# Keys and values of an attention context by seven half-block products instead of eight (f32, one Trainium2 core)

## The chip, the cores and the metric

The kernel runs on one core of one Trainium2 chip. The metric is the time on the device in microseconds (us), as the median of several runs. All arithmetic is f32.

## What is computed

A block of a network with cross attention, for one sequence of T = 4096 rows, H = 512 features, 8 heads of 64, and a context of S2 = 3202 rows. Cut to what matters:

```
x      = layernorm(builder_state); base_n = layernorm(ctx)            # rows of 512
q      = x @ Wq.T + bq;  k = base_n @ Wk.T + bk;  v = base_n @ Wv.T + bv
attn   = softmax(q k^T / 8) per head;  x = residual + (attn v) @ W_o.T + b_o
U      = (layernorm(x) @ W_in.T + b_in) @ Bmat
s_t    = silu(s_{t-1} @ A.T) + U_t                                    # a scan over t
result = x + s @ Cmat + mean(program_probs) @ W_prog.T + b_prog
```

The change touches only how k and v are formed: two products of the normalized context (3202 x 512) with 512 x 512 weights.

## The kernel before

The program has a first stage, which forms keys and values of the whole context and writes them to the chip's memory (`kd`, `vd`), and a long second stage, the attention and all that follows, whose instructions stand in an order that a planner wrote out by hand-set costs and due times (`Plan`). The second stage loads keys and values back in pieces (`load_k`, `load_v`, in SyncE's DMA queue, called SP).

In the first stage the context is cut into 26 chunks of 128 rows (the last has 2 rows), and the chunks into groups of GC = 4, so 512 keys a group. There are six full groups, 0 to 5, and a seventh with chunks 24 and 25.

- `load_chunk` (L566) loads a chunk by an SP DMA into `cx`, a ring of six.
- `norm_chunk` (L573) normalizes it: statistics on VectorE, three small operations on GpSimd, then one ScalarE instruction that writes `xh` (L288).
- `turn_chunk` (L592) transposes `xh` by four TensorE transposes into PSUM and copies them into `ct`, the group's 128 x 4 x 512 tile of features by keys: with VectorE for odd chunks, with ScalarE for even ones.
- For the first two chunks of groups 2 to 5 (`flips`, L605) TensorE is spared: `flip_pair` transposes 32 x 32 blocks on VectorE into a tile `pair`, and `move_pair` puts them in their place in `ct` by 16 SP DMAs, in four parts of four (L562).
- Values: for each chunk, four matmuls of 512 columns into a PSUM bank `pv` (L673), a ScalarE copy to `vs`, a store to `vd`.
- Keys: after a group's last chunk, for each of the four head pairs, four matmuls of 512 columns (all keys of the group) into a bank `pk` (L709), a ScalarE copy with bias to `ks`, two stores to `kd`.

PSUM has two banks each for `pk`, `pv` and the transposes. Each engine, and SP's queue, works through its instructions in the order in which the program gives them.

Beside this runs `side()` (a generator, `work`): weight preparation, row biases, and the first block of queries (`first_queries`). `next(work)` lets it run to its next `yield`; the code places these calls between the chunks and the key blocks, 70 of them, where 52 are enough to finish.

Of the kernel before, what the change touches and what calls it, by code (L numbers as in the profile page):

```python
# [10 lines left out]
F32 = mybir.dt.float32  # L11
BF16 = mybir.dt.bfloat16
I32 = mybir.dt.int32
AF = mybir.ActivationFunctionType
ALU = mybir.AluOpType
# [40 lines left out]
def keys(c):  # L56


    return CK if c < NCH - 1 else REST


def blocks(c):

    return 2 if c < NDC - 1 else 1


def key0(c):
    return c * CK


class Plan:
# [22 lines left out]
    def __init__(self, rings, held):  # L94
        self.rings = rings
        self.taken = {r: list(held.get(r, ())) for r in rings}
        self.pieces, self.givers = {}, {}
# [94 lines left out]
def xattn_ssm_kernel(  # L192
# [219 lines left out]
    def gain(k, w, i=None):  # L412
        for i in range(NC) if i is None else (i,):
            nc.vector.tensor_scalar(
                w[:, i, :], raw[k][:, i, :], g1s[:, i : i + 1], None, ALU.mult
            )
# [29 lines left out]
    def side():  # L446
# [14 lines left out]
        nc.scalar.dma_start(cb, ctxb[:a, :].rearrange("(p c) d -> p c d", p=P))  # L461
        cb2 = wp.tile([S2 - a, NS], F32, name="cb2")
        nc.scalar.dma_start(cb2, ctxb[a:, :])
        x0 = wp.tile([P, NT, H], F32, tag="raw_v", name="x0")
        yield

        nc.vector.tensor_scalar(bias[:, :NC], bias[:, :NC], HD**-0.5, None, ALU.mult)
# [47 lines left out]

        sums = wp.tile([P, NS], F32, name="sums")
        nc.vector.tensor_reduce(sums, cb.rearrange("p c d -> p d c"), AX.X, ALU.add)
        nc.scalar.dma_start(x0, x[:QB, :].rearrange("(t p) h -> p t h", p=P))
        yield
        pm = m_tile([P, 512], "pm")  # L520
# [45 lines left out]
    def load_chunk(c):  # L566
        if c < NCH:
            n = keys(c)
            xt = cin.tile([CK, H], F32, tag="cx", name=f"cx_{c}", bufs=6)
            nc.sync.dma_start(xt[:n], ctx_in[key0(c) : key0(c) + n, :])  # L570
            cxs[c] = xt

    def norm_chunk(c):  # L573
        if c < NCH:
            xhs[c] = normalize(cxs.pop(c), keys(c), f"c{c}", pool=cin)
# [16 lines left out]
    def turn_chunk(c):  # L592
        if c < NCH:
            g, n = c // GC, keys(c)
            if c % GC == 0:
                cts[g] = ctp.tile([P, NC, GC * CK], F32, tag="ct", name=f"ct_{g}")
            o = key0(c) - key0(g * GC)
            copy = nc.vector.tensor_copy if c % 2 else nc.scalar.copy
            tp = transposes(kps, "t", xhs.pop(c), n, f"c{c}")
            for cs in (slice(0, 2), slice(2, NC)) if c == 0 else (slice(0, NC),):  # L600
                copy(cts[g][:, cs, o : o + n], tp[:, cs])  # L601
# [3 lines left out]
    def flips(c):  # L605
        return FLIPS <= c // GC < NCH // GC and c % GC < 2

    def flip_pair(c):
        g = c // GC
        pairs[g] = wp.tile([P, NC, H], F32, tag="raw_" + "vqkq"[g - FLIPS], name=f"pair_{g}")  # L610
        for t in range(2):
            flip(pairs[g][:, :2], xhs.pop(c + t), t)

    def move_pair(c, *parts):
        g = c // GC
        if 0 in parts:
            cts[g] = ctp.tile([P, NC, GC * CK], F32, tag="ct", name=f"ct_{g}")
        for a in parts:
            move(cts[g][:, :, : 2 * CK], pairs[g][:, :2], a)

    with tc.manual_schedule():
        load_chunk(0)
        nc.scalar.dma_start(g1s, g1)
        fetch_w(2, nc.scalar, slice(0, NC // 2))
        fetch_w(2, nc.sync, slice(NC // 2, NC))
        load_chunk(1)
        load_chunk(2)
        fetch_w(1, nc.sync)
        load_chunk(3)
        idle = m_tile([P, 512], "idle")  # L630
        nc.scalar.copy(bu, neg_half)
        for _ in range(11):
            nc.tensor.matmul(idle[:, :P], a_t, a_t, start=True, stop=True)
        for t, src in ((be1s, beta1), (bqkv, b_qkv), (g2s, g2), (be2s, beta2)):
            nc.sync.dma_start(t, src)
        for c in range(4, 6):
            load_chunk(c)
        early = [first_chunk(c) for c in range(2)]
        next(early[0])
        next(early[0])  # L640
        turn_chunk(0)
        gain(2, wv, 0)
        gain(2, wv, 1)
        next(early[1])
        gain(2, wv, 2)
        norm_chunk(2)
        gain(2, wv, 3)
        next(early[1])
        work = side()
        first = shift(1)  # L650
        loads = [partial(load_k, *steps[k]) for k in range(AHEAD_K - 1)]
        loads += [partial(load_v, *steps[k]) for k in range(AHEAD - 1)]
        for c in range(NCH):
            load_chunk(c + 6)
            if c >= 2 * AHEAD_K:
                for _ in range(4):
                    if loads:
                        loads.pop(0)()
            if not flips(c + 3):
                norm_chunk(c + 3)  # L660
            elif c % GC == 1:
                norm_chunk(c + 3)
                norm_chunk(c + 4)
            if flips(c + 1) and c % GC == GC - 1:
                move_pair(c + 1, 0, 1)
            g, n = c // GC, keys(c)
            ct, o = cts[g], key0(c) - key0(g * GC)
            pv = kps.tile([P, 512], F32, tag="v", name=f"pv_{c}")
            parts = 1 if c < NCH - 1 else 2
            for i in range(NC // parts):  # L670
                for h in range(parts):
                    k = h * NC // parts + i
                    nc.tensor.matmul(  # L673
                        pv[h * HD : h * HD + n, :H],
                        ct[:, k, o : o + n],
                        wv[:, k, :],
                        start=(i == 0),
                        stop=(i == NC // parts - 1),
                        skip_group_check=True,
                    )  # L680
            if c == 0:
                turn_chunk(1)
            if not flips(c + 2):
                turn_chunk(c + 2)
            elif c % GC == 2:
                flip_pair(c + 2)
            if c < NCH - 1:
                vs = cin.tile([CK, NC, P], F32, tag="vs", name=f"vs_{c}")
                nc.scalar.copy(vs, pv)
                nc.sync.dma_start(vd[:, c // 2, :, c % 2, :].rearrange("h p d -> p h d"), vs)  # L690
            else:
                second = wp.tile([n, H], F32, name="second")
                nc.scalar.copy(second, pv[HD : HD + n])
                nc.vector.tensor_tensor(vx[:n], pv[:n], second, ALU.add)
                nc.sync.dma_start(vx[HD : HD + n], vx[:n])
            if c < GC:
                if c == 1:
                    gain(1, wk)
                for _ in range((0, 0, 1, 2)[c]):
                    next(first)  # L700
            else:
                next(work, None)
            if c % GC < GC - 1 and c < NCH - 1:
                continue
            n_g = o + n
            for hp in range(NC):
                pk = kps.tile([P, 512], F32, tag="k", name=f"pk_{g}_{hp}")
                for i in range(NC):
                    nc.tensor.matmul(  # L709
                        pk[:, :n_g],  # L710
                        wk[:, i, hp * P : (hp + 1) * P],
                        ct[:, i, :n_g],
                        start=(i == 0),
                        stop=(i == NC - 1),
                    )
                ks = cin.tile([P, GC * CK], F32, tag="ks", name=f"ks_{g}_{hp}")
                nc.scalar.activation(  # L717
                    ks[:, :n_g], pk[:, :n_g], AF.Identity, bias=bias[:, NC + hp : NC + hp + 1]
                )
                for b in range(g * GC, c + 1, 2):  # L720
                    m, k = blocks(b // 2) * CK, key0(b) - key0(g * GC)
                    nc.sync.dma_start(kd[hp, b // 2, :, :m], ks[:, k : k + m])
                if g == 0:
                    nc.gpsimd.tensor_copy(kx[:, hp, REST:], ks[:, : HD - REST])
                elif c == NCH - 1:
                    nc.gpsimd.tensor_copy(kx[:, hp, :REST], ks[:, CK : CK + REST])
                if hp < 2 and flips(c + 1):
                    move_pair(c + 1, 2 + hp)
                for _ in range(2 if g > 1 else 1):
                    next(work, None)  # L730
        left = sum(1 for _ in work)
        assert left == 0, left
    prep.close()
# [208 lines left out]
    def join(w):  # L942
        o = rows_of(w, o_t[w["at"]])
        nc.vector.tensor_tensor(o, rows_of(w, w["po"][1][:, :QU], True), o, ALU.add)
# [1080 lines left out]
```

## Time and profile before

| | us |
|---|---|
| median of 3 timed runs (1939.45, 1939.58, 1941.25) | 1939.58 |
| span of the profiled execution, first to last instruction | 1938.7 |
| the profiled execution's own time | not given apart from its span; the median lies 0.9 above the span |
| first stage, from the trace: first values' matmul, first scores | 7.5, 213.1 |
| 200 of the values' matmul instructions, busy | 90.4 |
| 192 + 32 of the keys' matmul instructions, busy | 85.1 + 3.8 |

PE is TensorE's matmuls, PEld its weight loads, DVE is VectorE, ACT is ScalarE, POOL is GpSimd, SP is SyncE, whose queue issues most DMAs. A matmul's duration in the trace includes the drain of the array and overlaps the next, so its price is read from the distance between starts. In a row of instruction groups the columns are line, engine, operation, tiles written and read, shapes, count, then busy time and mean duration in ns, then the idle time of the engine ahead of them with what ended it. A row of a timeline has the start, the length (us), the engine, the line and the count of merged instructions.

### The profile page before, as it was taken

How to read it: one execution, taken by the hardware profiler on the slowest of the kernel's cores; microseconds unless marked ns; L12 is line 12 of the kernel's file. 1: busy time of each engine (PE TensorE's matmuls, PEld its weight loads, DVE VectorE, ACT ScalarE, POOL GpSimd, SP SyncE). 2: the span in 40 equal slices, each digit the busy share in tenths (PEclk: the TensorE clock that was granted, in tenths of full speed). 3: DMA queues.
4: the chain of work that ended last, by engine and by line, in shares of the span. 5: the costliest groups of instructions: out<-in, count | busy, mean ns of one | idle time of the engine just before them, and what ended most of it. 6: DMA issues, size and time to landing. Idle time of an engine off the chain costs nothing.

```text
span 1938.7 us, 66985 instructions
## 1 busy us (share of the span) xinstructions
PE 1922.7 (99%) x29056; PEld 1275.0 (66%) x29056; DVE 1467.1 (76%) x1986; ACT 1169.3 (60%) x1626; POOL 217.2 (11%) x370
## 2 busy tenths in 40 slices
PE   9999999999999999999999999999999999999997
PEld 5444579676667666666667666766666666766675
DVE  5320489688877887888868887888788886978876
ACT  3232577576666666667657666666666765766653
POOL 2121000001200120002100120012000110011105
PEclk9999999999999999999999999999999999999999
DMA  6644234123432243233412343224323341545577
GB/s 198 196 120 113 64 87 115 47 87 88 125 87 81 84 119 77 68 96 83 124 49 87 88 126 84 82 83 120 76 73 92 81 123 58 150 115 145 171 190 227
DMA packets 260758, 207.43 MB, mean 107 GB/s; under 512 B 94632, under 2 KB 233896, under 8 KB 260460
## 3 DMA queue, kind: packets, MB, share of 16 engines
q1 hardware_dynamic: 256440, 196.48, 35.6%
q10 hardware_dynamic: 4020, 6.62, 1.1%
q8 instruction: 230, 3.77, 0.8%
q14 instruction: 68, 0.56, 0.1%
HBM read 156.32 MB, written 29.88 MB: 96 GB/s over the span
## 4 chain that ended last, share of the span: by engine, by line


## 5 line engine op out<-in xcount | busy, mean ns | idle before, releaser
L838 ACT ACTIVATE p<-s,shifts 128x1024 f32<-128x1024 f32 (+1 forms) x832 | 892.9, 1082 | 477.2 <-PE s L761 461.7
L846 DVE TENSOR_TENSOR acc<-p,acc 128x1024 f32<-128x1024 f32 (+1 forms) x704 | 828.6, 1177 | 136.2 <-ACT p L838 100.3
L761 PE MATMUL s<-q,k 64*64 64x256 f32 x12800 | 840.0, 377 | 0.2 <-ACT p L838 0.2
L895 PE MATMUL po<-p,v 64*64 64x256 f32 x12800 | 838.5, 377 | 0.0
L761 PEld LDWEIGHTS s<-q,k 64*64 64x64 f32 x12800 | 500.8, 133 | 198.9 <-ACT p L838 15.0
L895 PEld LDWEIGHTS po<-p,v 64*64 64x64 f32 x12800 | 498.0, 133 | 184.1 <-issue 17.5
L967 DVE RECIPROCAL rd<-rd 128x256 f32<-128x256 f32 (+1 forms) x64 | 110.1, 1722 | 70.9 <-ACT rd L962 70.9
L1132 POOL TENSOR_TENSOR xr<-xr,rowb 128x512 f32<-128x512 f32 x30 | 39.9, 1340 | 994.9 <-DMA xr<-in_x_dram 573.4
L333 PE MATMUL pq<-xn,wq 128*128 128x512 f32 x248 | 110.6, 598 | 0.0
L1138 PE MATMUL pa<-wo,o 128*128 128x512 f32 x240 | 107.0, 599 | 0.0
L673 PE MATMUL pv<-wv,ct 128*128 128x512 f32 (+1 forms) x208 | 92.2, 595 | 0.9 <-DVE ct L601 0.5
L709 PE MATMUL pk<-ct,wk 128*128 128x512 f32 (+1 forms) x224 | 88.9, 550 | 0.0
L846 DVE TENSOR_TENSOR acc<-p,p 128x1024 f32<-128x1024 f32 x64 | 80.3, 1254 | 10.1 <-ACT p L838 9.8
L333 PEld LDWEIGHTS pq<-xn,wq 128*128 128x128 f32 x248 | 45.7, 190 | 55.3 <-issue 55.3
L1138 PEld LDWEIGHTS pa<-wo,o 128*128 128x128 f32 x240 | 44.4, 190 | 56.0 <-issue 56.0
L601 DVE COPY ct<-tp_c 128x512 f32<-128x512 f32 (+1 forms) x9 | 5.7, 630 | 91.7 <-PE tp_c L304 91.7
L709 PEld LDWEIGHTS pk<-ct,wk 128*128 128x128 f32 x224 | 39.5, 190 | 44.5 <-issue 44.5
L673 PEld LDWEIGHTS pv<-wv,ct 128*128 128x128 f32 (+1 forms) x208 | 37.0, 186 | 44.5 <-issue 41.7
L342 ACT ACTIVATE q<-pq,bias 128x512 f32<-128x512 f32 x31 | 21.3, 688 | 73.3 <-PE pq L333 73.3
L717 ACT ACTIVATE ks<-pk,bias 128x512 f32<-128x512 f32 (+1 forms) x28 | 18.0, 642 | 72.5 <-PE pk L709 60.8
L870 DVE TENSOR_TENSOR acc<-swap,acc 64x256 f32<-64x256 f32 x126 | 53.0, 421 | 8.5 <-ACT swap L865 6.8
L865 ACT COPY swap<-acc 64x256 f32<-64x256 f32 x126 | 50.8, 403 | 7.3 <-DVE acc L853 3.9
(220 smaller groups left out, 1210.8 us busy)
## 6 DMA issues: line engine op xcount, KB each, us to landing
k<-kd SPq DMA_DIRECT2D x432, 128.0 KB, 2.3
v<-vd SPq DMA_DIRECT2D x432, 128.0 KB, 2.2
xn<-x SPq DMA_DIRECT2D x448, 32.0 KB, 1.9
xr<-in_x_dram SPq DMA_DIRECT2D x30, 256.0 KB, 3.3
x1d<-xr SPq DMA_DIRECT2D x30, 256.0 KB, 2.2
x<-in_x_dram SPq DMA_DIRECT2D x28, 256.0 KB, 3.3
cx<-in_ctx_dram SPq DMA_DIRECT2D x25, 256.0 KB, 2.9
vd<-vs SPq DMA_DIRECT2D x25, 256.0 KB, 2.5
```

Of the source, the lines that this page charges most:

```text
L333: nc.tensor.matmul(pq, wq[:, i, hp * P : (hp + 1) * P], xn[:, i, :], start=(i == 0), stop=(i == NC - 1),)
L673: nc.tensor.matmul(pv[h * HD : h * HD + n, :H], ct[:, k, o : o + n], wv[:, k, :], start=(i == 0), stop=(i == NC // parts - 1), skip_group_ ...
L709: nc.tensor.matmul(pk[:, :n_g], wk[:, i, hp * P : (hp + 1) * P], ct[:, i, :n_g], start=(i == 0), stop=(i == NC - 1),)
L761: nc.tensor.matmul(s[k0 : k0 + HD, a, b, :], kts[(*w["at"][:2], c)][r, b * CK + k0 : b * CK + k0 + HD], q[r], start=True, stop=True, skip_ ...
L838: nc.scalar.activation(t[:, :, :nb, :], w["ps"][c][:, :, :nb, :], AF.Exp, bias=w["shift"])
L846: nc.vector.tensor_tensor(w["acc"][:, :, :nb, :], t[:, :, :nb, :], before[:, :, :nb, :], ALU.add)
L865: nc.scalar.copy(w["swap"][r], of[(1 - k) * HD : (2 - k) * HD])
L870: nc.vector.tensor_tensor(of[r], w["swap"][r], of[r], ALU.add)
L895: nc.tensor.matmul(w["po"][k][a * HD : (a + 1) * HD, :QU], vts[Q, hp, c][r, b, a * HD : (a + 1) * HD], t[r, a, b, :], start=(c == 0 and b ...
L967: nc.vector.reciprocal(w["rd"][:, part], (w["pd"] if last else w["rd"])[:, part])
L1132: nc.gpsimd.tensor_tensor(v["x"], v["x"], rowb, ALU.add)
L1138: nc.tensor.matmul(v["pa"], o_t[Q, c, half][:, t * P : (t + 1) * P], wo[:, c, :], start=(c == 0), stop=(c == NC - 1),)
```

## The change

Groups 1 to 5 form keys and values by one level of Strassen's scheme (in Winograd's form). The 512 x 512 weight and the group's 512 x 512 tile are each seen as four quarters of 256 x 256 (`quarters`). Seven products of quarters and of sums of quarters give what eight products of quarters gave.

- `weight_sums` forms four sums of quarters for each weight, once, on GpSimd, in tiles of the attention's input rings. `key_sums` forms four sums of quarters of `ct` for each group on VectorE, in the ring of the queries' tiles; keys and values share them.
- A product (`Seven.product`) is four matmuls of 256 columns. Its results stay in two PSUM banks, `x` and `y`, which several products add to in turn.
- `keep` copies `x` to SBUF by ScalarE (keys: two instructions with bias; values: one). `join` adds `y` to that copy by VectorE, reading PSUM. `store` writes the finished quarter out: keys with one DMA, values with two.
- The 14 products of a group (seven for keys, a = 0, and seven for values, a = 1) stand in 14 slots in a fixed order, and the loads, norms, turns, moves and `next(work)` of the next group are hung on slots.
- Groups 0 and 6 keep the old products (`whole_chunk`, `whole_keys`). The next chunks are prepared at other places than before, `next(work)` stands at 59 places, the preloads for the second stage go out one in each slot of group 5, and the tile `x0` is taken just ahead of its load.

The diff, cut to its core:

```diff
+    def quarters(w):
+        lo, hi = slice(0, QU), slice(QU, H)
+        return w[:, :2, lo], w[:, 2:, lo], w[:, :2, hi], w[:, 2:, hi]
+    def weight_sums(w, pair):
+        a11, a12, a21, a22 = quarters(w)
+        s1, s2, s3, s4 = (t.rearrange("p (c o) -> p c o", c=2) for two in pair for t in (two[:, 0], two[:, 1]))
+        nc.gpsimd.tensor_tensor(s1, a21, a22, ALU.add)
+        nc.gpsimd.tensor_tensor(s2, s1, a11, ALU.subtract)
+        nc.gpsimd.tensor_tensor(s3, a11, a21, ALU.subtract)
+        nc.gpsimd.tensor_tensor(s4, a12, s2, ALU.subtract)
+        return dict(zip("1234567", (a11, a12, s4, a22, s1, s2, s3)))
+    def key_sums(ct, g):
+        b11, b21, b12, b22 = quarters(ct)
+        t1, t2, t3, t4 = (
+            qp.tile([P, QB], F32, tag="q", name=f"t{k}_{g}").rearrange("p (c k) -> p c k", c=2) for k in range(4)
+        )
+        nc.vector.tensor_tensor(t1, b12, b11, ALU.subtract)
+        nc.vector.tensor_tensor(t2, b22, t1, ALU.subtract)
+        nc.vector.tensor_tensor(t3, b22, b12, ALU.subtract)
+        nc.vector.tensor_tensor(t4, b21, t2, ALU.subtract)
+        return dict(zip("1234567", (b11, b21, b22, t4, t1, t2, t3)))
+    class Seven:
...
+        def product(self, k):
+            to, left, right = self.y if k in "235" else self.x, self.left[k], self.right[k]
+            for b in range(2):
+                of = slice(b * P, (b + 1) * P)
+                for i in range(2):
+                    nc.tensor.matmul(
+                        to[:, b, :],
+                        left[:, i, of] if self.of_keys else right[:, i, of],
+                        right[:, i, :] if self.of_keys else left[:, i, :],
+                        start=(k in "125" and b == 0 and i == 0),
+                        stop=(i == 1),
+                        skip_group_check=True,
+                    )
+        def keep(self, k, half):
...
+            if not self.of_keys:
+                nc.scalar.copy(t, self.x)
+                return
+            for b in range(2):
+                hp = 2 * half + b
+                nc.scalar.activation(
+                    t[:, b], self.x[:, b], AF.Identity, bias=bias[:, NC + hp : NC + hp + 1]
+                )
+        def join(self, k):
+            t = self.kept[k]
+            nc.vector.tensor_tensor(t, self.y, t, ALU.add)
+        def store(self, k, half, pair):
+            t, c, hs = self.kept.pop(k), 2 * self.g + pair, slice(2 * half, 2 * half + 2)
+            if self.of_keys:
+                nc.sync.dma_start(kd[hs, c].rearrange("h p k -> p h k"), t)
+                return
+            for j in range(2):
+                nc.sync.dma_start(vd[2 * half + j, c], t[:, :, j * P : (j + 1) * P])
+        def step(self, k):
+            self.product(k)
+            if k == "1":
+                self.keep("11", 0)
+            elif k == "2":
+                self.join("11")
+                self.store("11", 0, 0)
+            elif k == "6":
+                self.keep("12", 0)
+            elif k == "7":
+                self.keep("22", 1)
+                self.join("22")
+                self.store("22", 1, 1)
+            elif k == "4":
+                self.keep("21", 1)
+                self.store("21", 1, 0)
+            elif k == "3":
+                self.join("12")
+                self.store("12", 0, 1)
...
+        right = key_sums(cts[1], 1)
+        order = [(a, k) for k in "1265" for a in range(2)]
+        order += [(0, "7"), (1, "7"), (0, "4"), (0, "3"), (1, "4"), (1, "3")]
+        at_norm = (0, 2, 5, 8)
+        for g in range(1, NCH // GC):
+            both = [Seven(True, sums["k"], right, g), Seven(False, sums["v"], right, g)]
+            c = (g + 1) * GC
+            moved = flips(c)
+            for slot, (a, k) in enumerate(order):
+                both[a].step(k)
+                if slot in at_norm:
+                    n = c + at_norm.index(slot)
+                    norm_chunk(n)
+                    load_chunk(n + 4)
+                if moved and slot == 3:
+                    flip_pair(c)
+                elif moved and slot in (5, 7, 9):
+                    move_pair(c, *((0, 1), (2,), (3,))[(slot - 5) // 2])
+                elif not moved and slot in (4, 6):
+                    turn_chunk(c + (slot - 4) // 2)
+                if slot in (9, 11):
+                    turn_chunk(c + 2 + (slot - 9) // 2)
+                if slot == 11 and g + 1 < NCH // GC:
+                    right = key_sums(cts[g + 1], g + 1)
+                if g == NCH // GC - 1 and loads:
+                    loads.pop()()
+                if slot % 3 != 1:
+                    next(work, None)
```

In group 0 the weights' sums are formed at chunk 1 (values) and ahead of the keys (keys), and the turns of chunks 6 and 7 and the norm of chunk 7 stand between the key blocks.

More of the change, by code (lines that the diff above doesn't have):

```diff
@@ L463, in side @@
         nc.scalar.dma_start(cb2, ctxb[a:, :])
-        x0 = wp.tile([P, NT, H], F32, tag="raw_v", name="x0")
         yield
@@ L517, in side @@
         nc.vector.tensor_reduce(sums, cb.rearrange("p c d -> p d c"), AX.X, ALU.add)
+        x0 = wp.tile([P, NT, H], F32, tag="raw_v", name="x0")
         nc.scalar.dma_start(x0, x[:QB, :].rearrange("(t p) h -> p t h", p=P))
@@ new lines, in xattn_ssm_kernel, with __init__ @@
+    class Seven:
+        def __init__(self, of_keys, left, right, g):
+            self.of_keys, self.left, self.right, self.g = of_keys, left, right, g
+            tag = "k" if of_keys else "v"
+            self.x, self.y = (
+                kps.tile([P, 512], F32, tag=tag, name=f"p{tag}{k}_{g}").rearrange("p (b k) -> p b k", b=2)
+                for k in "xy"
+            )
+            self.kept = {}
+        def product(self, k):
[12 more added lines that the diff above has]
+        def keep(self, k, half):
+            t = cin.tile(
+                [P, 2, QU], F32, tag="ks" if self.of_keys else "vs", name=f"{'ks' if self.of_keys else 'vs'}_{self.g}_{k}"
+            )
+            self.kept[k] = t
+            if not self.of_keys:
[5 more added lines that the diff above has]
+                    t[:, b], self.x[:, b], AF.Identity, bias=bias[:, NC + hp : NC + hp + 1]
+                )
+        def join(self, k):
[27 more added lines that the diff above has]
+                self.store("12", 0, 1)
@@ new lines, in whole_chunk @@
+    def whole_chunk(c):
+        g, n = c // GC, keys(c)
+        ct, o = cts[g], key0(c) - key0(g * GC)
+        pv = kps.tile([P, 512], F32, tag="v", name=f"pv_{c}")
+        parts = 1 if c < NCH - 1 else 2
+        for i in range(NC // parts):
+            for h in range(parts):
+                k = h * NC // parts + i
+                nc.tensor.matmul(
+                    pv[h * HD : h * HD + n, :H],
+                    ct[:, k, o : o + n],
+                    wv[:, k, :],
+                    start=(i == 0),
+                    stop=(i == NC // parts - 1),
+                    skip_group_check=True,
+                )
+        yield
+        if c < NCH - 1:
+            vs = cin.tile([CK, NC, P], F32, tag="vs", name=f"vs_{c}")
+            nc.scalar.copy(vs, pv)
+            nc.sync.dma_start(vd[:, c // 2, :, c % 2, :].rearrange("h p d -> p h d"), vs)
+        else:
+            second = wp.tile([n, H], F32, name="second")
+            nc.scalar.copy(second, pv[HD : HD + n])
+            nc.vector.tensor_tensor(vx[:n], pv[:n], second, ALU.add)
+            nc.sync.dma_start(vx[HD : HD + n], vx[:n])
+        yield
@@ new lines, in whole_keys @@
+    def whole_keys(g, hp):
+        last = min(NCH, (g + 1) * GC) - 1
+        ct, n_g = cts[g], key0(last) - key0(g * GC) + keys(last)
+        pk = kps.tile([P, 512], F32, tag="k", name=f"pk_{g}_{hp}")
+        for i in range(NC):
+            nc.tensor.matmul(
+                pk[:, :n_g],
+                wk[:, i, hp * P : (hp + 1) * P],
+                ct[:, i, :n_g],
+                start=(i == 0),
+                stop=(i == NC - 1),
+            )
+        ks = cin.tile([P, GC * CK], F32, tag="ks", name=f"ks_{g}_{hp}")
+        nc.scalar.activation(
+            ks[:, :n_g], pk[:, :n_g], AF.Identity, bias=bias[:, NC + hp : NC + hp + 1]
+        )
+        for b in range(g * GC, last + 1, 2):
+            m, k = blocks(b // 2) * CK, key0(b) - key0(g * GC)
+            nc.sync.dma_start(kd[hp, b // 2, :, :m], ks[:, k : k + m])
+        if g == 0:
+            nc.gpsimd.tensor_copy(kx[:, hp, REST:], ks[:, : HD - REST])
+        elif last == NCH - 1:
+            nc.gpsimd.tensor_copy(kx[:, hp, :REST], ks[:, CK : CK + REST])
@@ L652, in xattn_ssm_kernel @@
         loads += [partial(load_v, *steps[k]) for k in range(AHEAD - 1)]
-        for c in range(NCH):
+        loads.reverse()
+        sums, right = {}, None
+        for c in range(GC):
             load_chunk(c + 6)
[L655 to L680, printed above, removed]
@@ L681, in xattn_ssm_kernel @@
+            norm_chunk(c + 3)
+            chunk = whole_chunk(c)
+            next(chunk)
             if c == 0:
                 turn_chunk(1)
[L683 to L701, printed above, removed]
-                next(work, None)
[L703 to L730, printed above, removed]
@@ new lines, in xattn_ssm_kernel @@
+            turn_chunk(c + 2)
+            next(chunk)
+            if c == 1:
+                gain(1, wk)
+                sums["v"] = weight_sums(wv, [xp_.tile([P, 2, H], F32, tag="x", name=f"sv_{k}") for k in range(2)])
+            for _ in range((0, 0, 1, 2)[c]):
+                next(first)
+        sums["k"] = weight_sums(
+            wk, [xp_.tile([P, 2, H], F32, tag=tag, name=f"sk_{tag}", bufs=1) for tag in ("x1", "xn2")]
+        )
+        for hp in range(NC):
+            whole_keys(0, hp)
+            if hp % 2:
+                load_chunk(10 + hp // 2)
+                turn_chunk(6 + hp // 2)
+            elif hp == 0:
+                norm_chunk(7)
+            next(work, None)
@@ new lines, in xattn_ssm_kernel @@
+        right = key_sums(cts[1], 1)
[25 more added lines that the diff above has]
+                if slot % 3 != 1:
+                    next(work, None)
@@ L731, in xattn_ssm_kernel @@
+        for c in range(NCH // GC * GC, NCH):
+            for _ in whole_chunk(c):
+                pass
+            next(work, None)
+        for hp in range(NC):
+            whole_keys(NCH // GC, hp)
+            for _ in range(2):
+                next(work, None)
+        while loads:
+            loads.pop()()
         left = sum(1 for _ in work)
```

## The prediction

> **What bounds the kernel now.** I read the page first: the engines, the 40 slices and the clock.
>
> ```profile
> span 1938.7 us, 66985 instructions
> PE 1922.7 (99%) x29056; PEld 1275.0 (66%) x29056; DVE 1467.1 (76%) x1986; ACT 1169.3 (60%) x1626; POOL 217.2 (11%) x370
> PE   9999999999999999999999999999999999999997
> PEclk9999999999999999999999999999999999999999
> ```
>
> TensorE is busy from end to end at full granted clock, so only fewer or shorter matmuls, or new idle time, can move the end. An average says nothing of one stage, so next come the stretches of the stage that the change touches, and who made TensorE wait there.
>
> ```profile
> core 0: us, PE busy (x) PEld busy (x) DVE busy (x) ACT busy (x) POOL busy (x), PEclk, DMA share, GB/s
> 20.00:40.00 20.00, 20.00 (x66) 10.34 (x65) 12.25 (x24) 5.12 (x8) 3.56 (x9) 1.00 0.48 146
> 140.00:160.00 20.00, 20.00 (x54) 9.20 (x53) 4.94 (x11) 7.53 (x12) 4.20 (x12) 1.00 0.45 119
> ```
>
> ```profile
> PE pm L523 <- DVE sums L517: 0.7, 1, 0.7
> PE sm L781 <- ACT ks L717: 0.2, 1, 0.2
> ```
>
> These two lines are TensorE's whole list of waits from 20 to 214 us: 0.9 us. The stage is bound by TensorE, and a microsecond taken from its matmuls ends the kernel a microsecond sooner unless something else comes late. The attention that follows keeps its own order and is TensorE-bound too; it just starts earlier. The page's chain of waits is empty here, so the bound rests on these views.
>
> **The matmuls.** "Busy" hides pipelining; the price of a matmul is the distance between starts, from the timeline of TensorE.
>
> ```profile
> 150.19 10.46 PE L709 MATMUL pk<-ct,wk 128*128 128x512 f32 x24
> 160.49 0.60 PE L304 MATMUL tp_x<-ident,xh_x 128*128 128x128 f32 x4
> 160.93 3.60 PE L709 MATMUL pk<-ct,wk 128*128 128x512 f32 x8
> ...
> 209.32 3.84 PE L709 MATMUL pk<-ct,wk 128*128 128x130 f32 x32
> 213.09 0.64 PE L781 MATMUL sm<-q,kx 64*64 64x256 f32 x2
> ```
>
> 24 instructions from 150.19 to 160.49 are 0.429 us each at 512 columns; four from 160.49 to 160.93 are 0.109 at 128; 32 from 209.32 to 213.09 are 0.118 at 130 (with the start of a new block in it). The next two rows give the counts and the weight loads.
>
> ```profile
> L709 PE MATMUL pk<-ct,wk 128*128 128x512 f32 x192 | 85.1, 595 | 0.0
> L709 PEld LDWEIGHTS pk<-ct,wk 128*128 128x128 f32 x224 | 39.5, 190 | 44.5 <-issue 44.5
> ```
>
> 192 instructions at 512 columns for six groups of 16 calls: an f32 matmul in the code is two instructions. No full-array matmul of 256 columns is in the trace. The straight line through 128 and 512 columns gives 0.109 + 128 x (0.429 - 0.109)/384 = 0.216 us; the same slope from the 130-column row gives 0.118 + 0.105 = 0.223. I take 0.216, because the stretches at 128 and 512 columns stand inside running work, and keep 0.223 as the dear end; half of 0.429 (0.215) is the cheap end.
>
> A group of 512 keys has 16 calls for keys and 16 for values before: 64 instructions x 0.429 = 27.5 us. After, 14 products of four calls with 256 columns: 112 x 0.216 = 24.2 us (25.0 at 0.223). That saves 3.3 us (2.5), and for five groups **16.3 us** (12.4). The number of weight loads rises from 64 to 112 a group; the 32 instructions at 130 columns carry the same 128x128 load and ran at 0.118, so a load keeps up with 0.216.
>
> The row above has 0.429 with a load of 0.190 for every matmul, so full-array loads lie beside the matmuls. The Trainium skill ("TensorE: Matmul & The Clock Gate", Part 3, The mechanism) says that a weight load overlaps running matmuls only when the row group differs. By that, each instruction would cost its load too, which at 512 columns the trace contradicts; what it would do to the new ones is the last rival below.
>
> **What is added beside them.** The rows for the new operations:
>
> ```profile
> L288 ACT ACTIVATE xh_c<-cx,nmr_c,rstd_c 128x512 f32<-128x512 f32 x23 | 18.3, 813 | 18.4 <-POOL nmr_c L280 17.8 <-DMA cb<-in_ctxb_2048x_dram 0.5
> L717 ACT ACTIVATE ks<-pk,bias 128x512 f32<-128x512 f32 x24 | 16.5, 687 | 70.1 <-PE pk L709 58.4 <-DMA modb<-in_L_xattn_b_prog_dram 5.4 <-DMA ct<-pair 4.0
> L689 ACT COPY vs<-pv 128x512 f32<-128x512 f32 x25 | 14.6, 586 | 37.9 <-PE pv L673 32.7 <-issue 5.3
> L823 ACT ACTIVATE x<-sm,shifts 128x256 f32<-128x256 f32 x4 | 1.7, 471 | 3.4 <-DMA v<-vd 3.2 <-DVE shifts L817 0.2
> L540 DVE TENSOR_TENSOR modb<-pr,modb 128x512 f32<-128x512 f32 x1 | 0.7, 692 | 3.7 <-PE pr L538 3.7
> L853 DVE TENSOR_TENSOR acc<-acc 128x512 f32<-128x512 f32 x1 | 0.7, 691 | 0.0
> L1132 POOL TENSOR_TENSOR xr<-xr,rowb 128x512 f32<-128x512 f32 x30 | 39.9, 1340 | 994.9 <-DMA xr<-in_x_dram 573.4
> ```
>
> VectorE gets six joins out of PSUM (0.692) and four key sums (0.691) a group: 6.9 us, hidden under 24 us of matmuls, since it is busy 4.9 of 20 us there. ScalarE goes from 4 x 0.687 + 4 x 0.586 = 5.1 us to 8 x 0.47 + 4 x 0.586 = 6.1, hidden likewise (7.5 of 20). Neither costs anything by its sum; order is the question below. PSUM banks are freed in time: product 4 of the keys needs `keep` of "22", and the products between leave 1.73 us or more (a product is 8 x 0.216 = 1.73). The stores are 12 DMAs a group before and after. The preloads of the attention's first tiles move from chunks 20 on into the last group's slots, one each, ahead of chunks 24 and 25 and the last keys; they read groups stored long before. Queries finish a little later, still ahead of the scores: nothing. If those covers failed, the attention would start late by a load's landing, 2.3 us.
>
> GpSimd forms the eight weight sums, 1.34 each, in two blocks of 5.4 us in the first group, ahead of the small steps that normalize chunks 5 and 7:
>
> ```profile
> 20.81 0.36 POOL L276 TENSOR_SCALAR ve_c<-mv_c 128x1 f32<-128x1 f32 x1 [5.20 <-DVE mv_c L269]
> 24.73 0.60 PE L304 MATMUL tp_c<-ident,xh_c 128*128 128x128 f32 x4
> ```
>
> GpSimd sat idle for 5.20 us before 20.81, where the first block just fits, and the transposes of chunk 5 come only at 24.73. So the least is nothing. The most: if GpSimd and VectorE slow one another, chunk 5 is late by up to one block less that cover, some 4 us. I take **0.5**, near the free row.
>
> **The order at a group's end.** This is what the saving must pay for. Chunks 8, 9, 12, 13, 16, 17, 20 and 21 are turned by VectorE and moved by 16 DMAs (`move_pair`). Before, a moved pair's last DMAs went out two key blocks and a value block (some 10 us) ahead of their first use. Now the very first product of the next group (b11 of keys) needs all 16, and the last four are issued in slot 9, behind both stores of "22". Call E the end of slot 8 (keys' product 7):
>
> ```profile
> 116.12 0.65 DVE L267 BATCH_NORM_STATS2 st_c<-cx 128x6 f32<-128x512 f32 x1
> 118.41 0.81 ACT L288 ACTIVATE xh_c<-cx,nmr_c,rstd_c 128x512 f32<-128x512 f32 x1
> 124.56 0.54 SPq L690 DMA_DIRECT2D vd<-vs  x1
> 129.87 2.52 SPq L562 DMA_DIRECT2D ct<-pair  x4
> 54.60 7.62 SPq L562 DMA_DIRECT2D ct<-pair  x8
> DMA to landing us min/median/max: 1.9/1.9/5.6
> ```
>
> - ScalarE `keep` of the keys, two of 0.47 after a drain of about 0.25: E+1.2. VectorE `join` 0.69: E+1.95.
> - `norm_chunk` of slot 8 is queued next. VectorE's statistics wait behind that join, and from statistics to the scaled write took 118.41 - 116.12 = 2.3 us: ScalarE scales from E+4.2 to E+5.0.
> - In ScalarE's queue stands, behind it, `keep` of the values' product 7 (its product is done at E+1.7): E+5.6. Join: E+6.3.
> - In SP's queue, behind that join: two value stores at about 0.45, then move 3, four DMAs of 0.63: the last goes out at E+9.1 and lands 1.9 later: **E+11.1**.
>
> TensorE meanwhile has slots 9 to 13 and two chunk transposes: 5 x 1.73 + 2 x 0.44 = **9.5 us**. So a new wait of 1.6 us stands at the start of the next group, less what `work` puts on TensorE after slot 8:
>
> ```profile
> L491 PE MATMUL pt<-twice,wct 128*128 128x64 f32 x8 | 1.0, 268 | 0.0
> L504 PE MATMUL pb<-bi,bm 128*64 128x1 f32 x8 | 0.6, 200 | 0.0
> L538 PE MATMUL pr<-rowv,ones 128*128 128x512 f32 x2 | 1.0, 592 | 0.0
> ```
>
> Group 1 has pt and two such pb blocks there (about 2 us: no wait if DMAs land in 1.9, but this is where landings were long, so 1.0); group 2 has pr (0.75); group 3 nothing (1.6); group 4 an extra 0.8 on ScalarE and one transpose (1.85). Group 5 is followed by chunks that are not moved. Sum: **5.2 us**. Bounds: 0 if the queue runs looser than I lined it up; 8 if group 1 lands a few microseconds late. Who waits behind: the next group's key sums, with 6.9 us (four slots) to spare, so TensorE stops once at each boundary, not twice.
>
> Sum on the profiled execution: 1938.7 - 16.3 + 5.2 + 0.5 = 1928.1. The timed runs' median, 1939.58, lies 0.9 above that span; carried over, **1929.0**.
>
> **The rivals.**
> - *The whole saving.* Each step of the chain above can be off by tenths; if they add up to 1.6 and `work` fills the rest, there are no waits: 1939.6 - 16.3 = 1923.3. For it: TensorE waited 0.9 us in 194. Against: that order left 10 us between last move and use.
> - *Starting a product is not free.* Compare two blocks of eight:
>
> ```profile
> 90.08 3.60 PE L709 MATMUL pk<-ct,wk 128*128 128x512 f32 x8
> 93.60 1.12 PE L538 MATMUL pr<-wp_t,mean 64*128 64x512 f32 x2
> 94.65 3.70 PE L709 MATMUL pk<-ct,wk 128*128 128x512 f32 x8
> ```
>
>   The one that follows a short matmul is 0.1 longer. With 0.1 at each of 70 products the saving falls by 7, and the longer products hide all but some 1.5 of the waits: 1939.6 - 16.3 + 7 + 1.5 + 0.5 = 1932.3. For: short matmuls leave less time to load ahead. Against: the stage's long rows show no such loss at chunk starts.
> - *Slower: the moves are the bound.* SP's queue at the boundary decides. If moves behave as in the row at 54.60 (0.95 each) and land in 5.6, move 3 is in at 7.2 + 3 x 0.95 + 5.6 = E+15.7: waits of about 6.2 at four boundaries less 3 of `work`, 22, against 16.3: 1939.6 + 6 = 1945.6. It decides from E+13.6 on (4 us a boundary). For: those are rows of this stage. Against: the median landing is 1.9, and the slow ones fall in the weight loads' time. The Trainium skill (the same page, Part 1) says that TensorE's clock halves after an idle window of about 3.4 us. Idle stretches of 6 us would then cost some 1.7 us each again, 1952 as an estimate; the stage before has no gap long enough to show it.
> - *Loads no longer hidden.* If a load of 0.190 lay beside a matmul of 0.429 but not beside one of 0.216, 112 x 0.190 = 21.3 us a group would come in: 1939.6 + 5 x (24.2 + 21.3 - 27.5) = 2029.6. The 0.118 of the 130-column row speaks against it.
> - *Between*: some of the first four, 1935.7 to 1943.5, no change that a measurement can tell.
>
> That fewer matmuls run than the change says, or more, I exclude: the list of slots holds 14 products of four calls.
>
> **How the numbers follow.** A measurement here can tell about 0.2% (3.9 us) from no change. Forecast 0.48; whole saving 0.25; product starts 0.12; between 0.06; moves as the bound 0.08; loads not hidden 0.01. So faster 0.85, same 0.06, slower 0.09. The range goes from the whole saving less the old 0.9 us of waits, 1922.4, to 1936.5, which holds the product starts and the dear matmul (0.223: 3.9 more); left out are the slower cases and the upper part of the between.
>
> **What would show it.** New matmuls 0.216 apart; five groups of about 24 us of products; a wait of TensorE on `ct<-pair` of 1 to 2 us at the start of groups 2 to 5, and `keep` of the values' "22" right after a scaled chunk on ScalarE. Wrong if the products start over 0.245 apart (27.5/112, where nothing is saved), if TensorE waits on `keep`, `join` or key sums inside a group, or if waits on the moves pass 4 us.

## The result, and the profile after

The changed kernel takes 1950.51 us (median of four runs, 1950.28 to 1950.85) against 1939.54 before (a fourth run moved that median by 0.04): ratio 1.0054, 95% interval 1.004 to 1.0068. It is 11 us slower where 10.6 us faster was forecast. The profiled execution took 1950.85 us with a span of 1949.0.

The page of the changed kernel, the rows that answer to those of before (engines, the slices of TensorE and of its clock):

```profile
span 1949.0 us, 67563 instructions
PE 1917.1 (98%) x29296; PEld 1326.3 (68%) x29296; DVE 1507.9 (77%) x2036; ACT 1171.9 (60%) x1646; POOL 230.5 (12%) x378
PE   8899999999999999999999999999999999999997
PEclk9899999999999999999999999999999999999999
```

TensorE's busy time fell by 5.6 us although the span grew, and the second slice of its clock is no longer full. All of the loss lies in the first stage: the attention's first score matmul (`s`) starts at 224.3 us in place of 214.0, and from there to the end it is 1724.7 us in both traces.

```profile
213.98 0.43 PE L761 MATMUL s<-q,k 64*64 64x256 f32 x1
...
224.30 0.43 PE L899 MATMUL s<-q,k 64*64 64x256 f32 x1
```

The list of TensorE's waits in the first 235 us (total, count, longest) is now the one below. From 20 us on it comes to 16.2 us, which was 0.9 before; 0.4 us of the line `tp_c` lie ahead of 20 us.

```profile
PE pkx L665 <- DMA ct<-pair: 5.2, 3, 2.4
PE pb L432 <- DVE shift L423: 3.5, 1, 3.5
PE pt L490 <- DVE wct L486: 3.0, 1, 3.0
PE pb L507 <- DVE wcr L495: 3.0, 1, 3.0
...
PE tp_c L304 <- ACT xh_c L288: 1.2, 2, 0.8
PE tp_x L304 <- ACT xh_x L288: 0.7, 1, 0.7
```

The first line is the wait that the prediction worked out: three stops, the longest 2.4 us. The next three were not in it: the side work's small matmuls, all in group 1. Each waits for a tile that VectorE writes one step of the side work earlier: `shift` (a weighted sum of the query weights), `wct` and `wcr` (copies of products of `W_in` and `Bmat` out of PSUM). The timeline of TensorE shows what stands behind such a wait:

```profile
42.64 1.89 PE L665 MATMUL pkx<-ct,wk 128*128 128x256 f32 x8
48.02 1.84 PE L432 MATMUL pb<-ones,shift 128*128 128x1 f32 x8 [3.48 <-DVE shift L423]
49.72 3.76 PE L665 MATMUL pvx<-wv,ct 128*128 128x256 f32 x8
53.27 2.53 PE L665 MATMUL pky<-ct,wk 128*128 128x256 f32 x8
55.64 1.89 PE L665 MATMUL pvy<-wv,ct 128*128 128x256 f32 x8
57.37 1.89 PE L665 MATMUL pkx<-t,sk_x 128*128 128x256 f32 x8
```

From 55.64 to 57.37 a product takes 1.73 us for eight instructions, 0.216 each: the price of the prediction, to the digit. But the first product behind the wait takes 3.55 us (49.72 to 53.27) and the second 2.37. In stretches cut to them, the figure behind POOL's busy time is the granted clock (PEclk):

```profile
47.70:54.60 6.90, 6.58 (x20) 5.62 (x21) 3.45 (x7) 1.40 (x2) 1.06 (x3) 0.51 0.39 133
54.60:75.00 20.40, 17.37 (x85) 13.79 (x84) 6.40 (x14) 4.74 (x9) 3.16 (x9) 1.00 0.77 197
75.00:78.40 3.40, 3.40 (x10) 2.70 (x9) 0.69 (x1) 1.76 (x4) 0.00 (x0) 0.51 0.67 218
85.30:92.10 6.80, 6.68 (x22) 5.50 (x23) 2.60 (x12) 0.00 (x0) 0.22 (x1) 0.50 0.00 1
177.40:180.80 3.40, 3.40 (x9) 2.72 (x9) 3.29 (x6) 0.55 (x2) 0.00 (x0) 0.51 0.44 132
```

TensorE ran at half speed for 6.8 + 3.4 + 6.8 + 3.4 = 20.5 us, each time behind a wait of 2.4 us or more. Half speed for 20.5 us is 10.2 us lost, 10.0 without the part in which TensorE stood still anyway.

The account of the stage's 10.3 us closes when every matmul is priced by the distance to the next start, with waits and half speed taken out. The matmuls of keys and values take 160.2 us in place of 175.7: -15.5, where 16.3 was worked out. Waits: +5.2 on the moves, +9.5 in the side work, +1.5 on chunk 5 and a query transpose, less the old 0.9: +15.2 before rounding. Half clock: +10.0. All other matmuls: +0.6.

### The profile page after: what moved, and what is told of

It is laid out like the page before. It is cut to its first block, busy times and chain, and to the rows that moved or that the text cites. A ratio compares the mean times of both kernels' runs of the same rounds, so it can differ in the third digit from the quotient of the medians.

```text
span 1949.0 us, 67563 instructions
## 1 busy us (share of the span) xinstructions
PE 1917.1 (98%) x29296; PEld 1326.3 (68%) x29296; DVE 1507.9 (77%) x2036; ACT 1171.9 (60%) x1646; POOL 230.5 (12%) x378
## 5 line engine op out<-in xcount | busy, mean ns | idle before, releaser
L984 DVE TENSOR_TENSOR acc<-p,p 128x1024 f32<-128x1024 f32 x64 | 79.3, 1239 | 10.2 <-ACT p L976 9.8
L288 ACT ACTIVATE xh_c<-cx,nmr_c,rstd_c 128x512 f32<-128x512 f32 (+1 forms) x24 | 19.5, 813 | 62.4 <-POOL nmr_c L280 62.4
L970 DVE TENSOR_TENSOR acc<-x,acc 2x256 f32<-2x256 f32 x128 | 53.1, 415 | 2.6
L1293 POOL TENSOR_TENSOR xr<-x,modb 128x512 f32<-128x512 f32 x30 | 38.2, 1274 | 118.2 <-DVE x L1289 118.2
L684 ACT ACTIVATE ks<-pkx,bias 128x256 f32<-128x256 f32 x40 | 16.8, 471 | 52.2 <-PE pkx L665 36.2
L690 DVE TENSOR_TENSOR ks<-pky,ks 128x512 f32<-128x512 f32 x15 | 10.4, 690 | 48.1 <-ACT ks L684 20.5
L991 DVE TENSOR_TENSOR acc<-acc 128x512 f32<-128x512 f32 x63 | 44.2, 701 | 1.4
```

Source lines behind the costliest of these rows:

```text
L970: nc.vector.tensor_tensor(to[r], t[r], to[r], ALU.add)
L984: nc.vector.tensor_tensor(w["acc"][:, :, :nb, :], t[:, :, :nb, :], before[:, :, :nb, :], ALU.add)
L991: nc.vector.tensor_tensor(acc[:, :, 0, :], acc[:, :, 0, :], acc[:, :, 1, :], ALU.add)
```

## Experiments

**Is the half clock a loss of its own?** Theory A: it follows the waits and costs what it lasts. Rival B: the slow stretches have another cause. Idle matmuls were put where TensorE waited:

```diff
+    def fill(to, n):
+        for _ in range(n):
+            nc.tensor.matmul(to, ident, ident[:, : to.shape[-1]], start=True, stop=True, skip_group_check=True)
...
+        if k == 0:
+            fill(pb[:, P : 2 * P], 8)
...
+            if k == "1" and self.of_keys and self.g > 1:
+                fill(to[:, 0, :P], {3: 4, 4: 8, 5: 8}.get(self.g, 0))
```

> The changed kernel with idle matmuls (128x128 on the identity, results overwritten) put in front of the six places where TensorE waited 0.9 to 3.5 us: 8 calls of 0.22 us ahead of the three waits of the side work in group 1, 4 or 8 ahead of the first product of groups 3, 4 and 5. The waits end when they ended before, so nothing else is sped up. Theory A (the clock falls after a wait and the half-speed stretches cost about 10.3 us by themselves): no gap over 1.8 us is left, the stretches are at full speed, 1950.5 - 10 = about 1940.5. Rival B (the slow stretches have another cause, such as loads of weights fighting with DMAs or VectorE for memory): they stay and the time is 1950.5 or a little more.

Measured: 1945.72 us, 1.0027 (1.0016 to 1.0038) of the kernel before, so 5 us less than the change with more matmuls in it. The half clock shrank from 20.5 to 6.8 us. It is half of what A expected: TensorE still waited 2.6 us for `wcr`, since the work ahead of that wait came sooner by more than VectorE's copy did (83.4 in place of 85.4 us), and 1.6 us for the query shift; behind these two the clock fell once each. B is out: two thirds of the half speed went with the waits. The forecast of A was too good because a filled wait moves the next one.

**The moves.** The prediction's chain has one link that can be taken out: the scaled chunk between the two `keep`s of product 7.

```diff
-        at_norm = (0, 2, 5, 8)
+        at_norm = (0, 2, 5, 7)
```

> The changed kernel with the fourth norm_chunk of a group at slot 7 in place of slot 8, so that the scaled chunk is no longer queued on ScalarE between the keys' and the values' keep of product 7. Theory (chain of the prediction: scaled chunk, keep, join, two stores, last four moves): the last move goes out some 2.5 to 3.5 us sooner and lands before slot 14, so the waits on the moves at groups 3, 4, 5 (5.2 us) and the half-speed stretch behind the last one (1.8 us) go: 1950.5 - 7 = 1943.5; the key sums of group 2 start sooner too, so that the third wait of the side work shrinks: down to 1938. Rival (the moves themselves or their landing are the bound, 16 DMAs of 0.64 us on SP): the waits shrink by less than half, 1947 or more.

Measured: 1939.37 us, 0.9995 (0.9986 to 1.0005). The whole list of TensorE's waits from 20 us on:

```profile
PE pb L507 <- DVE wcr L495: 4.2, 1, 4.2
PE pb L432 <- DVE shift L423: 3.5, 1, 3.5
PE pt L490 <- DVE wct L486: 2.2, 1, 2.2
PE tp_c L304 <- ACT xh_c L288: 0.8, 1, 0.8
```

No wait on `ct<-pair` is left, so the chain is the cause of those waits. At the end of group 3 it held to 0.4 us at every link; in the changed kernel it reads there (E is 136.84), on VectorE, ScalarE, SP and TensorE:

```profile
137.91 0.69 DVE L690 TENSOR_TENSOR ks<-pky,ks 128x512 f32<-128x512 f32 x1 [6.99 <-ACT ks L684]
...
140.86 0.81 ACT L288 ACTIVATE xh_c<-cx,nmr_c,rstd_c 128x512 f32<-128x512 f32 x1 [2.97 <-POOL nmr_c L280]
141.58 0.57 ACT L680 COPY vs<-pvx 128x512 f32<-128x512 f32 x1
...
144.18 2.61 SPq L562 DMA_DIRECT2D ct<-pair  x4
...
148.36 1.97 PE L665 MATMUL pkx<-ct,wk 128*128 128x256 f32 x8 [1.84 <-DMA ct<-pair]
```

The scale at E+4.0 (worked out: E+4.2), the values' `keep` right behind it, the next group's first product at E+11.5 (E+11.1 for the landing). The gain is 11 us where 7 to 12.5 were expected; the half clock fell from 20.5 to 13.7 us, partly because the `pt` wait, now 2.2 us, no longer lowers it. One part of the expectation failed: the third wait of the side work did not shrink but grew from 3.0 to 4.2 us. Group 2's key sums, which stand ahead of `wcr`, started 1.6 us sooner (80.82 in place of 82.41), but TensorE came to that wait 2.9 us sooner (79.59 in place of 82.45).

**The side work.** In the changed kernel these rows of VectorE, and one of ScalarE, stand ahead of the three waits (which end at 48.02, 73.42 and 85.42):

```profile
42.84 0.69 DVE L601 COPY ct<-tp_c 128x512 f32<-128x512 f32 x1 [7.25 <-PE tp_c L304]
43.45 1.67 DVE L414 TENSOR_SCALAR wq<-raw_q,g1s 128x512 f32<-128x512 f32 x4
...
45.55 2.32 DVE L423 SCALAR_TENSOR_TENSOR shift<-raw_q,be1s,shift 128x512 f32<-128x512 f32 x3
...
70.29 0.84 ACT L684 ACTIVATE ks<-pkx,bias 128x256 f32<-128x256 f32 x2 [6.90 <-DMA a_t<-in_L_xattn_A_dram]
...
71.22 0.69 DVE L690 TENSOR_TENSOR ks<-pky,ks 128x512 f32<-128x512 f32 x1 [9.95 <-DMA ct<-pair]
...
72.71 0.66 DVE L486 COPY wct<-pw 128x512 f32<-128x512 f32 x1
...
82.41 0.69 DVE L642 TENSOR_TENSOR t<-ct 128x512 f32<-128x512 f32 x1 [1.36 <-DMA ct<-pair]
...
84.95 0.42 DVE L495 COPY wcr<-pt 128x256 f32<-128x256 f32 x1
```

VectorE stood idle for 7.25 us at chunk 7's copy with the query weights' scaling and `shift` queued behind it, and for 9.95 us at a join with `wct` behind it. The row puts the second down to the moves, but the `keep` that this join adds to ended only at 70.29 + 0.84, and the join started 0.1 us later. That `keep` was itself late: its product was done at 68.2, and ScalarE's queue was issuing the side work's loads until 70.2. Ahead of `wcr` stand the key sums, which waited 1.36 us for the moves and took 2.5.

The edit puts each `next(work)` one step earlier, so that its VectorE operations are queued ahead of joins, chunk copies and key sums:

```diff
             whole_keys(0, hp)
+            next(work, None)
             if hp % 2:
...
-            next(work, None)
...
+                if slot % 3 != 1:
+                    next(work, None)
                 both[a].step(k)
...
-                if slot % 3 != 1:
-                    next(work, None)
```

> The changed kernel with every call of the side work one step earlier: ahead of its slot's product, and ahead of the turn of chunks 6 and 7 in group 0. So its VectorE operations stand ahead of the joins and key sums in VectorE's queue. Theory (the three waits of 3.5, 3.0 and 3.0 us in group 1 come from VectorE's order, and the half speed behind them costs 8.5): 1950.5 - 18 = 1932.5, with the waits on the moves left; a new wait of up to 2.5 us on the column sums (pm) in group 2 is possible, 1935. Rival (late DMAs of the side work's weights hold it up, whatever the order): the waits stay, 1947 or more.

Measured: 1934.14 us, 0.9968 (0.9956 to 0.9979): the expected 1932.5 to 1935. All three waits are gone and the moves remain. The new wait on the column sums is there too, with 6.8 us of half clock behind it that the expectation did not have:

```profile
PE pkx L665 <- DMA ct<-pair: 5.6, 4, 1.8
PE pm L523 <- DVE sums L516: 2.8, 1, 2.8
PE tp_c L304 <- ACT xh_c L288: 0.8, 1, 0.8
```

So the order of the queues made them wait, not late loads. This edit moves all three at once; the second and the third were not undone alone. The first cause alone, the step in group 0 ahead of chunk 7's copy (the first hunk of that diff):

> The changed kernel with one cause undone: in group 0 only, the side work's step ahead of the turns of chunks 6 and 7 and of the norm of chunk 7, so that the query weights' scaling stands ahead of chunk 7's copy on VectorE. Theory: the first wait (3.5 us) and the 6.8 us of half clock behind it (3.4) go and nothing else: 1950.5 - 6.9 = 1943.6. Rival (the wait is for the query weights' own load, not for the order): 1949 or more.

Measured: 1941.5 us, 1.0007 (0.9997 to 1.0016), 9 less than the change where 6.9 was expected. The 3.5 us wait and its half clock are gone; the clock also no longer fell behind the `pt` wait (2.3 us) nor behind the last wait on the moves (2.4), although these stayed. The wait for `wcr` grew to 4.4 us. The same waits lower the clock or not, which leads to the probe below.

**Both together.**

> Both edits, the fourth norm at slot 7 and the side work one step earlier. Theory (products save 16.3; all that was lost is waits on VectorE's queue, waits on the moves, and the half clock behind both): no wait over 1 us, 1950.5 - 18 - 7 = 1925.5, between 1923.5 and 1929. Rival (a part of the loss is in the products themselves or in the later attention): over 1932.

Measured: 1929.72 us, 0.995 (0.9933 to 0.9966), just outside the expected 1923.5 to 1929. One wait over 1 us was left, against the expectation: 2.6 us for the column sums, with 3.4 us of half clock behind it. Two idle steps of the side work take it away:

```diff
         nc.scalar.dma_start(x0, x[:QB, :].rearrange("(t p) h -> p t h", p=P))
-        yield
+        for _ in range(3):
+            yield
```

> Both edits of the run before (fourth norm at slot 7, side work one step earlier) and two idle steps of the side work between the column sums on VectorE and the matmul that reads them. Theory: the one wait of 2.6 us that was left on TensorE goes, and the half clock of 3.41 us behind it (1.7): 1929.7 - 4.3 = 1925.4. Rival (the later steps of the side work, moved back by two, now come late at the start of the attention): 1928 or more.

Measured: **1923.85 us** (1922.83 to 1927.68), 0.9918 (0.9904 to 0.9931) of the kernel before, which took 1939.67 beside it: 15.8 us faster, with an interval of 13 to 19. The profiled execution is the slowest of the five (1927.68). In it the first score matmul starts at 199.7 us in place of 214.0, 14.3 sooner; the matmuls of keys and values take 159.8 us in place of 175.7, 15.9 less. The clock is full through the stage, and this is all that TensorE waited for from 20 us on:

```profile
PE tp_c L304 <- ACT xh_c L288: 0.8, 1, 0.8
PE pvx L666 <- ACT vs L681: 0.8, 1, 0.8
PE pkx L666 <- DMA ct<-pair: 0.3, 1, 0.3
PE pkx L666 <- ACT ks L685: 0.2, 1, 0.2
```

**The last 0.8 us.** The value weights' sums on GpSimd were moved behind the norms of chunks 5 and 6:

> As the run beside it, and the sums of the value weights on GpSimd moved from chunk 1 to the place of the key weights' sums, behind the norms of chunks 5 and 6. Theory: the wait of 0.8 us for chunk 5 goes, 1924.6. Rival: the block of 11 us on GpSimd now makes chunk 7 late: the wait moves there, 1925.4 or up to 2 us more.

Measured: 1929.98 us, 0.9943 (0.9929 to 0.9956), 6 worse than without. The rival came true, at a higher price: the block ran on GpSimd from 25.6 to 37.3 us, chunk 7's scaling stood ahead of a key copy in ScalarE's queue, and TensorE waited for that copy's bank:

```profile
41.13 6.75 PE L754 MATMUL pk<-ct,wk 128*128 128x512 f32 x8 [3.34 <-ACT ks L762]
```

3.3 us, and 6.8 us of half clock behind it. The wait of 0.8 that it cured was cheaper because it was short.

**The clock by itself.**

> Not the kernel: a probe that leaves the whole computation out and writes zeros. TensorE runs streams of f32 matmuls of 256 columns (12, 15 or 18 calls, about 5.2, 6.5 and 7.8 us), and between them waits for a chain of ScalarE copies that is made longer and longer, so that it idles for about 1.0 to 4.3 us (eight lengths, three times each). Theory A (the clock is granted by windows of 3.41 us on a fixed grid, and a window that is idle for about half or more halves the next one): idle times up to about 1.5 us never lower the clock, those over 3.5 us always do, and between them it depends on how the idle time falls on the grid, not on its length alone; each low stretch lasts 3.41 or 6.83 us. Rival B (a fixed idle time sets it, from the trace between 1.84 and 2.42 us): all idle times over one length lower the clock and none under it.

The timeline of TensorE in the probe, two pieces of it (the gap ahead of each stream in brackets):

```profile
44.33 5.45 PE L37 MATMUL p<-row,ident 128*128 128x256 f32 x24 [1.80 <-ACT row L41]
52.02 7.13 PE L37 MATMUL p<-row,ident 128*128 128x256 f32 x24 [2.25 <-ACT row L41]
61.86 7.13 PE L37 MATMUL p<-row,ident 128*128 128x256 f32 x24 [2.70 <-ACT row L41]
...
142.15 6.74 PE L37 MATMUL p<-row,ident 128*128 128x256 f32 x30 [2.70 <-ACT row L41]
```

24 instructions take 5.45 us at full clock and 7.13 behind a gap of 2.25 or 2.70; 30 take 6.74, full clock, behind another gap of 2.70. The clock's own record has low stretches of 3.41 or 6.83 us, and they start whole multiples of 3.41 us apart. Laid on the grid of 3.41 us that this gives, the 24 gaps sort like this: gaps of 0.46 to 1.8 us never lowered the clock (10 of 10, the largest idle share of a grid window 0.53); gaps of 4.0 and 4.9 always did (5 of 5, 0.73 to 1.0); of 2.25, 2.70 and 3.15 us six of nine did, with shares of 0.58 to 0.76; the three that did not had 0.50, 0.53 and 0.57. So A holds and the fixed length of B falls: in this probe, with over about 0.57 of a 3.41 us window idle, TensorE ran at half speed for the next one or two windows. What makes it two is not shown.

## Why the prediction was wrong

- *Matmuls*: 0.216 us for 256 columns, measured 0.216; saving 16.3 worked out, 15.5 measured in the changed kernel and 15.9 in the repaired one. Full-array weight loads (0.190 us each) stayed hidden beside matmuls 0.216 apart, against the rule of the Trainium skill ("TensorE: Matmul & The Clock Gate", Part 3) that was weighed. A start of a product costs nothing behind another product or a chunk's transposes (1.73 us each) and 0.1 behind a block of the side work (1.83).
- *Moves*: 1.0 + 0.75 + 1.6 + 1.85 = 5.2 worked out; 0 + 0.96 + 1.84 + 2.42 = 5.2 measured; the sum is nearer than its terms, which is luck. Group 1's moves were not early but late: the key sums that need them started at E+14.3 where E+11.1 was worked out, and TensorE did not see it because the side work's waits had held it up. With the side work moved, a wait of 0.7 us appeared there.
- *GpSimd's sums*: 0.5 worked out, 0.8 measured, by the way that was named for the dear end: VectorE's scaling of the key weights ran beside the sums and took 3.66 us in place of 1.67, and chunk 5's statistics stood behind it.
- *The step that failed* is the cover: "less what `work` puts on TensorE after slot 8" counted the side work's matmuls as something that fills TensorE's time, and "Queries finish a little later, still ahead of the scores: nothing" was all that was said of its order. So the sum had nothing for its waits, and they took 9.5 us. I did not follow its VectorE halves through VectorE's queue, as I had done for the moves. Each has its matmul one step on, and in that queue now stand, ahead of them, chunk 7's copy (first wait), a join that waits for ScalarE (second), and key sums that wait for the moves (third). None of the signs listed as showing it wrong named the side work. VectorE was busy only 4.2 of the 20 us from 60 us on; what counts is what its head waits for.
- *The clock* had no term in the sum and was given only to the slower rival, at idle stretches of 6 us, after the Trainium skill (the same page, Part 1: half clock after an idle window of about 3.4 us). Here stops of 2.4 to 3.5 us paid for it. That added 10.0 us to 16.2 us of waits, and by the account above turned a kernel within 1 us of the old time into one 11 us slower. The slower rival ended on the right side by the wrong mechanism: the moves never took more than 2.4 us.
- That part of the saving goes at the group boundaries was right (three of the four cost a wait); that I summed only the waits of the new code, and none of the old code that the change re-queued, was the error.

## What to carry to other kernels

Where an engine is the bound at 99%, an edit that shortens its work is won or lost in the queues of the others: follow every instruction of the neighbours' side work, not only of the new code, to what stands ahead of it in its engine's queue. Keep a producer's vector half a few steps ahead of the matmul that reads it, and ahead of operations that wait for something late. Price a stop of TensorE in two parts: in these runs one of up to some 1.8 us cost its length (unless tiny matmuls followed it), a longer one could cost 1.7 or 3.4 us of half clock on top, so that spreading a wait, or filling it, is worth more than it looks.

## What was not expected of the hardware

- On the grid of 3.41 us a window need not be idle all through: in the probe 0.57 of a window idle left the clock full, 0.58 halved the next, and equal gaps of 2.70 us fell on both sides. Small matmuls seem to count as little work, though no run tests that alone: the clock also fell behind a window idle for only 0.47, where eight instructions of one column followed a gap of 1.61 us (the filled kernel, at 49.9 us), and for 0.53, where eight of 64 columns followed the `pt` wait (the changed kernel, at 75.0).
- GpSimd and VectorE can slow one another where both run 128x512 f32: GpSimd's sums took 1.27 to 1.72 us, and of VectorE's four scalings of the key weights the two beside them took 1.46 and 1.49 us, the two after them 0.48 each.
